# Layer 3 attention in steps of one key tile by eight heads, its halves split by token and turned just in time, TensorE in order

## The chip, the core and the metric

The kernel runs on one NeuronCore of a Trainium2 chip. Five engines work from queues of their own and meet at semaphores: TensorE (PE; its weight loads are listed as PEld), VectorE (DVE), ScalarE (ACT), GpSimd (POOL) and SyncE (SP, which issues DMAs). The metric is the device time of one execution in microseconds (us); smaller is better. Several executions give a median.

## The reference, cut to what matters

The program is four pairs of cross attention and feed-forward, run one after the other on x (4 batches of 256 tokens, 256 features) with a context of 4 x 1601 tokens. The change is in the last pair:

```python
def _L3_xattn_ref(x, context, Wq, Wk, Wv):        # 32 heads of 8
    q = (x @ Wq.T).reshape(b, n, 32, 8)
    kv = concatenate([context @ Wk.T, context @ Wv.T], -1).reshape(b, m, 32, 8, 2)
    k, v = kv[..., 0], kv[..., 1]
    q, k = _rmsnorm(q), _rmsnorm(k)               # over the 8 of a head
    attn = softmax(einsum('bhnd,bhmd->bhnm', q, k) * 8 ** -0.5)
    return einsum('bhnm,bhmd->bhnd', attn, v)
...
x = x + _L3_xattn_ref(_layernorm(x), ctx_2048, Wq, Wk, Wv)
x = x + _L3_ffn_ref(_layernorm(x), w_gate, w_up, w_down)
```

The feed-forward rounds weights to -1, 0, 1 and activations to whole numbers up to 127, and is 256 to 1024 to 256.

## The kernel before

P is 128 partitions, S 256 tokens, M 1601 context tokens in NM = 13 key tiles (the last of ML = 65 rows), B 4 batches, HD3 8.

**Heads on the array.** A head has only 8 features, so a score product uses 32 rows of the array: four runs of the head's 8, in which K and Q are split into a high part (upper bits) and the rest, so that the four pairs of parts are summed and the product keeps its accuracy in the fp32r type. Four heads lie in the four row groups of 32 and run side by side. `kT` and `qT` hold the normed K and Q turned to features by tokens, two tiles of 16 heads each (index `h`). For round `u` of four, `runs` (L1966 to L1974) takes 4 heads of the 16: a stream shuffle copies each head's 8 rows four times (L1971), two masks with per-partition bits make the part to subtract and the rest (L1972, L1973, VectorE), and GpSimd subtracts them into `kb` or `qb` (L1974). `spread` does so for a round in pieces of 256 columns, the next round's while this one runs.

**A step** is two key tiles by four heads (`pairs`, seven steps a round, the last of one tile). `scores` (L1987) makes eight products of 32 rows, 128 columns out and 256 tokens into two `s` tiles of 1024 columns (two PSUM banks each, three buffers go round), and ScalarE makes two exponentials `e` of them (L1998). `values` (L2002) multiplies the previous step's `e` by `va`: V with a column of ones after each head's 8, of which 32 columns are taken, in the four column groups side by side, into `o` (one buffer); these are plain fp32 and each appears as two matrix instructions in the trace. After a round, VectorE copies `o` to `os` (L2112), and `close` (L2012) turns it, divides by the sum that the ones gave, and GpSimd adds it to x (L2025).

**Side work.** `beside` (L2027) is a generator that the loop advances once a step: the K and V projection of the next batch (`l3_kv`, L1706: per key tile two fp32 products of 512 columns, four matrix instructions, then copies by VectorE; squares, norms; then the turning of all of K to `kT`, L1751), the next batch's queries (L1818), for batch 0 the rounding of the feed-forward weights (L1868), and the feed-forward of the batch before (`ffn`, L1911). They share one PSUM bank (`bank`, L1791). Batch 0's own K, V and `kT` are made during the layer 2 feed-forward; eleven key tiles of batch 1 while batch 0's queries are prepared (`FIRST3`). Layer 2's result is added to x for batches 1 to 3 by `l2_add` just before the loop, pinned on VectorE.

**Order.** The framework schedules every engine's queue from its own estimate; what is passed to `pin` (L118, `keep_in_program_order`) keeps its program order. In this stretch nothing of TensorE is pinned. All helper products are recorded under L79 (`mm`). The loop is L2082 to L2120; after it come the last `close` and the feed-forward of batch 3 (L2131 on).

Of the kernel before, what the change touches and what calls it, by code (L numbers as in the profile page):

```python
# [24 lines left out]
P = 128  # L25
# [32 lines left out]
VW3 = 16 * (HD3 + 1) + 24  # L58


class Kernel:
    def __init__(self, ctx, tc, ins, out):
        self.ctx, self.tc, self.nc = ctx, tc, tc.nc
        self.i, self.out = ins, out
        self.flip = 0
        self.hold = False
        self.flip4 = 0
# [10 lines left out]
    def mm(self, out, lhsT, rhs, start, stop, **kw):  # L78
        self.nc.tensor.matmul(out, lhsT, rhs, start=start, stop=stop, **kw)  # L79
# [1595 lines left out]
    def l3_open(self, es):  # L1675
# [4 lines left out]
        self.low3 = self.a3.tile([P, 2], I32, name="low3")  # L1680
        self.rest3 = self.a3.tile([P, 2], I32, name="rest3")
        nc.gpsimd.iota(self.low3, pattern=[[0, 2]], base=0, channel_multiplier=1)
        for n, bit in enumerate((4, 3)):
            c = self.low3[:, n : n + 1]
            nc.vector.tensor_scalar(c, c, 31 - bit, 31, ALU.logical_shift_left, ALU.arith_shift_right)
        nc.vector.tensor_scalar(self.rest3, self.low3, HIGH, None, ALU.bitwise_or)
        nc.vector.tensor_scalar(self.low3, self.low3, HIGH, None, ALU.bitwise_and)
# [9 lines left out]
    def values3(self, pool):  # L1697

        va = [pool.tile([P, NM, VW3], F32, name="va3", bufs=2) for _ in range(2)]
        n = 16 * (HD3 + 1)  # L1700
        for t in va:
            self.nc.vector.memset(t[:, :, :n].rearrange("p m (h e) -> p m h e", e=HD3 + 1)[:, :, :, HD3:], 1.0)
            self.nc.vector.memset(t[:, :, n:], 1.0)
        return va

    def l3_kv(self, b, st, early):  # L1706
# [4 lines left out]
        pool = self.late3 if b % 2 else self.a3  # L1711
        kr = st["kr"] = self.a3.tile([P, NM, D], F32, name="kr3")
        va = st["va"] = self.va3[b % 2]
        ss = st["ss"] = self.a3.tile([P, (NM + 2) * NH3 + 2], F32, name="ss3")
        for m in range(NM):
# [4 lines left out]
            tp = tf.rearrange("p (h d c) -> p h d c", d=HD3, c=2)  # L1720
            copy(kr[:, m, :].rearrange("p (h d) -> p h d", d=HD3), tp[:, :, :, 0])
            for h in range(2):
                copy(
                    va[h][:, m, : 16 * (HD3 + 1)].rearrange("p (h e) -> p h e", e=HD3 + 1)[:, :, :HD3],
                    tp[:, h * 16 : (h + 1) * 16, :, 1],
                )
# [15 lines left out]
        for _ in range(1 if b else 3):  # L1742
            yield
        kT = st["kT"] = [pool.tile([P, MP], F32, name="kT3", bufs=2) for _ in range(2)]
        for m0 in range(0, NM, 4):
            for h in range(2):
                n = min(4, NM - m0)
                copy = nc.scalar.copy if early() else nc.vector.tensor_copy
                tp = self.take().rearrange("p (m k) -> p m k", k=P)
                for m in range(n):  # L1750
                    nc.tensor.transpose(tp[:, m, :], kr[:, m0 + m, h * P : (h + 1) * P], self.ident)  # L1751
                copy(kT[h][:, m0 * P : (m0 + n) * P], tp[:, :n, :].rearrange("p m k -> p (m k)"))
                yield

    def l3_squares(self, st, v, m0, early, pool=None):

        n = v.shape[1]
        sq = pool.tile([P, 1, D], F32, name="sqq3", tag="run3", bufs=3) if pool else self.a3.tile([P, 5, D], F32, name="sq3")
# [9 lines left out]
    def l3(self, first):  # L1768
# [10 lines left out]
        pairs = [tuple(range(m, min(m + 2, NM))) for m in range(0, NM, 2)]  # L1779
        with ExitStack() as es:  # L1780
# [3 lines left out]
            ps_s = es.enter_context(tc.tile_pool(name="a3s", bufs=3, space=PSUM))  # L1784
            ps = es.enter_context(tc.tile_pool(name="a3p", bufs=1, space=PSUM))
            ps_o = es.enter_context(tc.tile_pool(name="a3o", bufs=1, space=PSUM))
            low, rest, idb = self.low3.bitcast(U32), self.rest3.bitcast(U32), self.idb
# [30 lines left out]
            def queries(b, st, old=None, fill=lambda n: None):  # L1818
# [13 lines left out]
                fill(0)  # L1832
                tp = bank().rearrange("p (k q t) -> p k q t", k=2, q=2)
                for k in range(2):
                    for q in range(2):
                        nc.tensor.transpose(tp[:, k, q, :], xn[:, q, k * P : (k + 1) * P], self.ident)
# [8 lines left out]
                qr = one.tile([P, 2, D], F32, name="qr3")  # L1845
# [12 lines left out]
                yield  # L1858
                yield
                qT = st["qT"] = two.tile([P, 2, S], F32, name="qT3")  # L1860
                tp = bank().rearrange("p (h t) -> p h t", h=2)
                for h in range(2):
                    for q in range(2):
                        nc.tensor.transpose(tp[:, h, q * P : (q + 1) * P], qr[:, q, h * P : (h + 1) * P], self.ident)
                nc.vector.tensor_copy(qT, tp)
# [45 lines left out]
            def ffn(b, q, xn, take):  # L1911
# [10 lines left out]
                yield  # L1922
                tp = take(BF16)[:, : 2 * P].rearrange("p (k t) -> p k t", k=2)
                for k in range(2):
                    nc.tensor.transpose(tp[:, k, :], vb[:, k * P : (k + 1) * P], idb)
                xT = two.tile([P, 2, P], BF16, name="xqT3")
                nc.vector.tensor_copy(xT, tp)
                yield
                g = two.tile([P, I3], F32, name="g3")
                for c in range(0, I3, 512):  # L1930
# [7 lines left out]
                    yield  # L1938
# [4 lines left out]
                    yield  # L1943
                hs, r = scale_of(g, "hq3")
                yield
                nc.vector.tensor_scalar(g, g, r, RND, ALU.mult, ALU.add)
                yield
# [3 lines left out]
                yield  # L1951
                tp = take(BF16).rearrange("p (k t) -> p k t", t=P)
                for k in range(I3 // P):
                    nc.tensor.transpose(tp[:, k, :], hb[:, k * P : (k + 1) * P], idb)
                hT = two.tile([P, I3 // P, P], BF16, name="hT3")
                nc.vector.tensor_copy(hT, tp)
                yield
# [8 lines left out]
            def runs(out, v, u, n):  # L1966

# [326 lines left out]
```

## Time and profile before

| | |
|---|---|
| median of 12 runs | 2521.85 us (2513.15 to 2528.69) |
| profiled execution | 2526.49 us |
| its span | 2524.8 us, 45207 instructions |
| whole span, busy | PE 2341.3, DVE 1636.6, ACT 1297.7, POOL 1018.0 us |
| mean granted TensorE clock | 0.963 |
| first score product / last exponential start | 1929.0 / 2494.0 us |

The stretch of this attention, cut so that each piece holds one round of four heads (14 exponentials of the tile `e` each), in us:

| batch | round 1 | 2 | 3 | 4 | 5 | 6 | 7 | 8 |
|---|---|---|---|---|---|---|---|---|
| 0 | 33.70 | 18.70 | 14.10 | 15.60 | 15.50 | 15.40 | 13.60 | 13.60 |
| 1 | 22.60 | 26.30 | 21.20 | 19.90 | 13.30 | 16.70 | 15.50 | 15.20 |
| 3 | 19.70 | 15.10 | 17.70 | 14.30 | 13.50 | 15.00 | 13.60 | 13.10 |

Costs of single instructions there, from its groups by shape: exponential of 1024 columns 1031 ns (of 512: 600 ns), mask of 256 columns 424 and 377 ns, shuffle 442 ns, GpSimd's subtraction of 256 columns 763 ns, scaling of `kr` 2077 ns, squares 2321 ns, ScalarE's table load 1283 ns (eleven of them), tanh 690 ns. How to read it: "busy" is the time in which an engine had at least one instruction; a wait is named with the instruction that waited, an arrow, and what released it.

### The profile page before, as it was taken

The page shows a single profiled execution, that of the slowest core. Times are in us where ns is not written, and L with a number is a line of the kernel's source. Part 1 is how long each engine was busy: PE and PEld are TensorE (multiplying, and loading weights), DVE is VectorE, ACT ScalarE, POOL GpSimd, SP SyncE. Part 2 cuts the span into 40 slices and gives each one's busy share as a digit, 9 for nine tenths or more (in the row PEclk, how much of TensorE's full clock was granted, in tenths as well). Part 3 has the DMA queues.
Part 4 walks back from the last instruction along what each step waited for, and adds up shares of the span by engine and source line. Part 5 has one row for each costly group of instructions (what it writes and reads, how often), then busy time and mean ns, then how long its engine had stood idle before and what let it go on. Part 6 is the DMA issues. An engine that isn't in the chain of part 4 may idle for free.

```text
span 2524.8 us, 45207 instructions
## 1 busy us (share of the span) xinstructions
PE 2341.3 (93%) x15959; PEld 1436.7 (57%) x15959; DVE 1636.6 (65%) x3940; ACT 1297.7 (51%) x3000; POOL 1018.0 (40%) x1773
## 2 busy tenths in 40 slices
PE   8989987899899999999999999998997898898897
PEld 5778876667645555555555555555563443444443
DVE  5553534753577777777777777773325876868774
ACT  3334444533655555445555454442324785857885
POOL 1015645312445555555555555542102544434331
PEclk9999998989999999999999999998998898998998
DMA  7165575633721111111111111004212000000000
GB/s 253 49 198 172 172 150 158 215 98 110 221 66 48 49 48 48 49 48 48 48 49 48 43 43 47 22 1 170 87 67 67 18 18 28 4 3 2 6 6 5
DMA packets 96521, 188.33 MB, mean 75 GB/s; under 512 B 15450, under 2 KB 64346, under 8 KB 95099
## 3 DMA queue, kind: packets, MB, share of 16 engines
q1 hardware_dynamic: 80150, 146.50, 17.5%
q0 software_dynamic: 10416, 28.46, 5.0%
q10 hardware_dynamic: 5732, 10.49, 1.3%
q8 instruction: 130, 2.13, 0.4%
q14 instruction: 93, 0.75, 0.1%
HBM read 137.29 MB, written 48.11 MB: 73 GB/s over the span
## 4 chain that ended last, share of the span: by engine, by line
PE 74%; DVE 14%; issue 4%; POOL 3%; ACT 2%; DMA 2%; another core or an unknown queue 1%; SPq 0%; ACTq 0%; POOLq 0%; DVEq 0%
PE o L79 21%; PE s L79 18%; PE f2gu L79 3%; PE b L79 3%; PE f1gu L79 2%; PE f0gu L79 2%; PE acc L79 2%; PE fill L1260 2%; PE tpq L79 2%; PE tpkv L79 2%; PE av L79 2%; DVE hi L1972 2%; DVE run L1971 2%; PE f0y L79 2%; PE f2y L79 1%
## 5 line engine op out<-in xcount | busy, mean ns | idle before, releaser
L1520 ACT ACTIVATE p<-s,nmsm 128x448 f32<-128x448 f32 (+1 forms) x512 | 326.0, 643 | 372.6 <-PE s L79 243.4
L1998 ACT ACTIVATE e<-s 128x1024 f32<-128x1024 f32 (+1 forms) x448 | 398.0, 970 | 143.7 <-PE s L79 141.9
L79 PE MATMUL o<-pT,va 128*128 128x256 f32 (+2 forms) x1920 | 430.2, 376 | 5.8 <-DVE pT L1561 4.3
L79 PE MATMUL s<-kT,qT 128*32 128x448 f32 (+1 forms) x4096 | 428.1, 556 | 7.9 <-ACT kT L1492 7.7
L79 PEld LDWEIGHTS o<-pT,va 128*128 128x128 f32 (+1 forms) x1920 | 344.1, 190 | 126.4 <-issue 86.2
L1555 POOL TENSOR_SCALAR p<-p,rm 128x448 f32<-128x448 f32 (+1 forms) x512 | 323.1, 651 | 6.3
L79 PE MATMUL o<-e,va 128*32 128x256 f32 (+1 forms) x3328 | 283.4, 410 | 27.1 <-DVE os L2112 21.1
L1516 DVE TENSOR_REDUCE nmsm<-s 128x2 f32<-128x896 f32 (+1 forms) x256 | 287.3, 1123 | 8.0
L1561 DVE STREAM_TRANSPOSE pT<-p 128x896 f32<-128x896 f32 (+1 forms) x256 | 270.6, 1111 | 4.7 <-POOL p L1555 4.0
L79 PEld LDWEIGHTS s<-kT,qT 128*32 128x32 f32 x4096 | 120.5, 109 | 260.3 <-issue 238.7
L1548 POOL TENSOR_TENSOR rm<-em,tot 32x8 f32<-32x8 f32 x256 | 54.1, 212 | 397.1 <-DVE tot L1545 385.8
L1974 POOL TENSOR_TENSOR kb<-run,hi 128x256 fp32r<-128x256 f32 (+1 forms) x224 | 155.4, 705 | 121.2 <-DVE run L1973 119.6
L79 PEld LDWEIGHTS o<-e,va 128*32 128x32 f32 (+1 forms) x3328 | 105.8, 113 | 121.7 <-ACT e L1998 30.2
L1513 DVE TENSOR_TENSOR s<-s,mask 128x128 f32<-128x128 f32 (+1 forms) x256 | 84.2, 330 | 99.7 <-PE s L79 91.6
L79 PE MATMUL s<-qb,kb 32*128 32x256 f32 (+1 forms) x1664 | 131.8, 346 | 17.5 <-ACT e L1998 11.7
L79 PEld LDWEIGHTS s<-qb,kb 32*128 32x128 f32 (+1 forms) x1664 | 77.4, 189 | 112.4 <-issue 61.9
L475 POOL DMA_INDIRECT f0xr<-f0xd,f0src x95 | 90.8, 955 | 68.9 <-PE f0y L79 24.4
L1260 PE MATMUL fill<-wkc_early,ctxT 128*128 128x256 f32 (+1 forms) x444 | 108.9, 396 | 9.4 <-ACT va_early L1268 7.2
L1520 ACT ACTIVATION_READ_ACCUMULATOR p<-s,nmsm 128x1 f32 x512 | 101.3, 198 | 0.0
L1972 DVE TENSOR_SCALAR hi<-run,low 128x256 uint32<-128x256 uint32 (+1 forms) x256 | 100.2, 410 | 0.2
L1260 PEld LDWEIGHTS fill<-wkc_early,ctxT 128*128 128x128 f32 (+1 forms) x444 | 85.7, 197 | 25.1 <-ACT va_early L1268 8.3
L1974 POOL TENSOR_TENSOR qb<-run,hi 128x256 fp32r<-128x256 f32 x32 | 25.8, 808 | 174.7 <-PE s L79 108.5
(518 smaller groups left out, 3935.7 us busy)
## 6 DMA issues: line engine op xcount, KB each, us to landing
ctxT<-in_ctxT SPq DMA_DIRECT2D x9, 1664.0 KB
vd<-va_early SPq DMA_DIRECT2D x96, 128.0 KB
kd<-kT_early SPq DMA_DIRECT2D x48, 256.0 KB
kT<-kd SPq DMA_DIRECT2D x16, 768.0 KB
va<-vd SPq DMA_DIRECT2D x16, 768.0 KB
f0yd<-f0ys SPq DMA_DIRECT2D x95, 128.0 KB
wq<-in_l_wq SPq DMA_DIRECT2D x16, 512.0 KB
wo<-in_l_wo SPq DMA_DIRECT2D x16, 512.0 KB
```

Of the source, the lines that this page charges most:

```text
L79: self.nc.tensor.matmul(out, lhsT, rhs, start=start, stop=stop, **kw)
L475: nc.gpsimd.indirect_dma_start(out=t, out_offset=None, in_=xd[:, :], in_offset=bass.IndirectOffsetOnAxis(ap=src[:, n : n + 1], axis=0),)
L1260: ins = nc.tensor.matmul(tp[:rows, t, :], ctxT[u // NKV2][:, k, c0 : c0 + rows], w[u % NKV2][:, k, :], start=k == 0, stop=k == 1,)
L1513: nc.vector.tensor_tensor(sv, sv, mask[:, 2 * c : 2 * c + 2, : nt - CT, :].rearrange("p n t i -> p n (t i)"), ALU.add)
L1516: nc.vector.tensor_reduce(ms[:, 0, 2 * c : 2 * c + 2], s[:, :, : nt * 32], AX.X, ALU.max, negate=True)
L1520: nc.scalar.activation(p[:, n, : nt * 32], s[:, n, : nt * 32], AF.Exp, bias=ms[:, 0, e : e + 1], accum_out=ms[:, 1, e : e + 1],)
L1548: nc.gpsimd.tensor_tensor(r[32 * a : 32 * a + 32], e[:, a], tot, ALU.mult)
L1555: nc.gpsimd.tensor_scalar(p[:, n, : nt * 32], p[:, n, : nt * 32], r[:, e : e + 1], 1.0, ALU.mult, ALU.mult)
L1561: self.pin(nc.vector.transpose(pT[:, 2 * c : 2 * c + 2, :nt, :].rearrange("p n t i -> p n (t i)"), p[:, :, : nt * 32]))
L1972: nc.vector.tensor_scalar(t.bitcast(U32), a.bitcast(U32), low[:, n : n + 1], None, ALU.bitwise_and)
L1974: nc.gpsimd.tensor_tensor(out, a, t, ALU.subtract)
L1998: nc.scalar.activation(e[:kr, :, :n, :], s[t][:kr, :, :n, :], AF.Exp, scale=1.0 / math.sqrt(HD3))
```

## The change

Weights are reordered on the host (`by_group`) so that a group `g` of eight heads is contiguous in a token's row, and V follows K instead of alternating with it. K and Q stay by token (`kr`, `qr`, two buffers each); `kT` and `qT` are gone. `halves` splits a part (three or four key tiles, eight heads, 64 features) into high part and rest, side by side, with one mask on VectorE and one subtraction on GpSimd. `turned` transposes it on TensorE, and for each `u` of two, VectorE shuffles the four runs out of PSUM and GpSimd copies them to the fp32r tile. `feed` does the splitting one part ahead and the turning at the start of the part before. A step is one key tile by eight heads (`u` is now the inner index of the tiles `s` and `e`). `values` takes the 32 columns of `va` from two heads' 18 on, by `e` of both heads, 512 columns, into an `o` of 512; of each half of the columns the rows of one head are used. `close` covers eight heads. PSUM: `s` two buffers, the bank two, `o` two. `self.strict` pins all of TensorE from the loop's start to its end. The side work yields after each half of a key tile's projection, and a counter `room`, raised by RATE each step and lowered by turns, closings and units, says when it advances; the feed-forward's yields count 0.5 and end the step's share. The functions `runs`, `spread` and the masks by partition bits are removed.

```diff
+VW3 = 16 * (HD3 + 1) + 14
+PARTS = [(0, 4), (4, 7), (7, 10), (10, NM)]
+RATE = [1.2, 1.5, 1.5, 0.8]
...
     def mm(self, out, lhsT, rhs, start, stop, **kw):
-        self.nc.tensor.matmul(out, lhsT, rhs, start=start, stop=stop, **kw)
+        self.ordered(self.nc.tensor.matmul(out, lhsT, rhs, start=start, stop=stop, **kw))
+    def ordered(self, ins):
+        if self.strict:
+            self.pin(ins)
...
         for m in range(NM):
             tf = self.take()
             for k in range(2):
                 self.mm(tf, ctxT[:, k, m * P : (m + 1) * P], self.wkv3[:, k, :], k == 0, k == 1)
...
+                if k == 0 and not early():
+                    yield
+            copy(kr[:, m, :], tf[:, :D])
+            copy(
+                va[:, m, :, : 16 * (HD3 + 1)].rearrange("p g (h e) -> p g h e", e=HD3 + 1)[:, :, :, :HD3],
+                tf[:, D:].rearrange("p (g h d) -> p g h d", g=2, d=HD3),
+            )
...
+        st["kr"] = kr
```

In the attention's function (indentation cut):

```diff
-ps_s = es.enter_context(tc.tile_pool(name="a3s", bufs=3, space=PSUM))
-ps = es.enter_context(tc.tile_pool(name="a3p", bufs=1, space=PSUM))
-ps_o = es.enter_context(tc.tile_pool(name="a3o", bufs=1, space=PSUM))
...
+ps_s = es.enter_context(tc.tile_pool(name="a3s", bufs=2, space=PSUM))
+ps = es.enter_context(tc.tile_pool(name="a3p", bufs=2, space=PSUM))
+ps_o = es.enter_context(tc.tile_pool(name="a3o", bufs=2, space=PSUM))
...
+def halves(v, g, name, bufs):
+    n = v.shape[1]
+    t = two.tile([P, n if bufs == 1 else 4, P], F32, name=name, bufs=bufs)[:, :n]
+    tv = t.rearrange("p n (e c d) -> p n e c d", c=2, d=HD3)
+    vv = v[:, :, g * 64 : (g + 1) * 64].rearrange("p n (e d) -> p n e d", d=HD3)
+    nc.vector.tensor_scalar(tv[:, :, :, 0, :].bitcast(U32), vv.bitcast(U32), HIGH, None, ALU.bitwise_and)
+    nc.gpsimd.tensor_tensor(tv[:, :, :, 1, :], vv, tv[:, :, :, 0, :], ALU.subtract)
+    return t
+def turned(out, t, order):
+    n = t.shape[1]
+    tp = bank()[:, : n * P]
+    for k in range(n):
+        self.ordered(nc.tensor.transpose(tp[:, k * P : (k + 1) * P], t[:, k, :], self.ident))
+    for u in range(2):
+        row = two.tile([P, 4 * P], F32, name="row3")[:, : n * P]
+        nc.vector.stream_shuffle(
+            row, tp, [16 * u + (k % 16 if order else k // 16 * 8 + k % 8) for k in range(32)]
+        )
+        nc.gpsimd.tensor_copy(out[:, u, : n * P], row)
+def feed():
+    last = None
+    for b in range(B):
+        for g in range(4):
+            for c, (m0, m1) in enumerate(PARTS):
+                st = states[b]
+                now = m0, c, halves(st["kr"][:, m0:m1, :], g, "half3", 2)
+                if c == 0:
+                    now += (halves(st["qr"], g, "halfq3", 1),)
+                if last is not None:
+                    yield ready(*last)
+                last = now
+    yield ready(*last)
+def ready(m0, c, t, tq=None):
+    k = two.tile([P, 2, 4 * P], F32R, name="kb3")
+    turned(k, t, True)
+    if c == 0:
+        self.q3 = two.tile([P, 2, S], F32R, name="qb3")
+        turned(self.q3, tq, False)
+    return k, self.q3, m0
...
+def scores(k, q, m):
     s = [ps_s.tile([P, 2, 2, S], F32, name="s3") for _ in range(2)]
...
+    kr = ML if m[0] == NM - 1 else P
+    c = (m[0] - m[1]) * P
+    for u in range(2):
         for r in range(4):
             rows = slice(32 * r, 32 * r + 32)
...
+            self.mm(s[r // 2][:kr, r % 2, u, :], k[rows, u, c : c + kr], q[rows, u, :], True, True)
...
+def values(e, o, va, g, m, b):
+    kr = ML if m == NM - 1 else P
+    for r in range(4):
+        c = (4 * r + g % 2 * 2) * (HD3 + 1)
+        self.mm(
+            o[32 * r : 32 * r + 32, :], va[:kr, m, g // 2, c : c + 32],
+            e[r // 2][:kr, r % 2].rearrange("p u t -> p (u t)"), m == 0, m == NM - 1,
+        )
+def close(b, os, g):
+    tp = bank()
+    for k in range(4):
+        self.ordered(nc.tensor.transpose(tp[:, k * P : (k + 1) * P], os[:, k * P : (k + 1) * P], self.ident))
```

Order of side work and the loop:

```diff
+        for _ in range(2 * (NM - sum(FIRST3) if b == 0 else NM)):
             next(kv)
             yield
         qs = queries(b + 1, st, b - 1 if b else None)
...
+        for _ in range(3):
             next(qs)
             yield
         for _ in kv:
...
+self.strict = True
+starts = [m0 for m0, _ in PARTS]
 last = done = None
 for b in range(B):
...
+    side = beside(b, states[b + 1] if b + 1 < B else {})
+    room = 0.0
+    for g in range(4):
+        o = ps_o.tile([P, 2 * S], F32, name="o3")
+        for m in range(NM):
+            room = min(room + RATE[b], 2.0)
+            if m in starts:
+                k, q, m0 = kq
+            e = scores(k, q, (m, m0))
+            if m == m0:
+                if b + 1 < B and g == 3 and m == starts[2]:
+                    while "qr" not in states[b + 1] or "kr" not in states[b + 1]:
                         next(side)
...
+                kq = next(more, None)
+                room -= 0.8
+            if m == 2 and done is not None:
                 close(*done)
                 done = None
...
+                room -= 0.8
+            while room > 0.5:
+                w = next(side, self)
+                if w is self:
+                    break
+                room -= w or 1.0
+                if w:
+                    break
+            if last is not None:
+                values(*last)
+                if last[4] == NM - 1:
+                    os = two.tile([P, 2 * S], F32, name="os3")
+                    nc.vector.tensor_copy(os, last[1])
+                    done = (last[5], os, last[3])
+            last = (e, o, states[b]["va"], g, m, b)
...
+self.strict = False
+values(*last)
+os = two.tile([P, 2 * S], F32, name="os3")
```

## The prediction

> **What bounds the kernel now.** I read the page first, then the layer 3 attention cut at the first exponential of each batch (112 exponentials each), then that stretch's waits, then single steps in the timeline. All that the change touches runs from 1929.0, the first score product, to 2495.3: 566.3 us of 2524.8.
>
> ```profile
> core 0: us, PE busy (x) PEld busy (x) DVE busy (x) ACT busy (x) POOL busy (x), PEclk, DMA share, GB/s
> 1929.00:2069.20 140.20, 119.43 (x1318) 57.66 (x1322) 117.42 (x396) 105.69 (x120) 65.41 (x92) 0.87 0.09 29
> 2069.20:2219.90 150.70, 134.28 (x1398) 63.31 (x1402) 112.05 (x387) 106.15 (x121) 60.35 (x88) 0.93 0.04 14
> 2219.90:2373.30 153.40, 136.49 (x1415) 64.52 (x1418) 114.67 (x392) 106.16 (x121) 60.83 (x88) 0.96 0.01 3
> 2373.30:2495.30 122.00, 111.70 (x1332) 52.42 (x1332) 75.63 (x290) 103.51 (x120) 40.36 (x70) 0.97 0.02 5
> ```
>
> One batch a row, batch 0 first. No engine is full: ScalarE does 105 us in each, and the batches take 122 to 153. TensorE (85 to 91% busy) and VectorE (84% in batch 0) share the limit, and it moves. In the waits of that stretch ScalarE waits for the score products, and TensorE for the copy that empties `o` (the weight loads wait for it too) and for `kb`:
>
> ```profile
> ACT e L1998 <- PE s L79: 141.9, 104, 4.9
> PE o L79 <- DVE os L2112: 21.1, 17, 2.4
> PEld s L79 <- POOL kb L1974: 20.0, 32, 4.2
> ```
>
> **The price of a step.** A full step now is two key tiles by four heads; the new one is one key tile by eight. Both have eight score products of 256 columns, two exponentials of 128x1024, and values over 2048 columns. Their rows on TensorE, in time order:
>
> ```profile
> 1972.45 0.51 PE L79 MATMUL s<-qb,kb 32*128 32x256 f32 x8
> 1972.89 1.07 PE L79 MATMUL o<-e,va 128*32 128x256 f32 x16
> 1973.89 0.66 PE L1751 MATMUL b<-ident,kr 128*128 128x128 f32 x4
> 1974.47 0.51 PE L79 MATMUL s<-qb,kb 32*128 32x256 f32 x8
> ...
> 2082.82 1.98 PE L79 MATMUL b<-wkv,ctxT 128*128 128x512 f32 x4
> 2084.73 0.51 PE L79 MATMUL s<-qb,kb 32*128 32x256 f32 x8
> ```
>
> From start to next start: scores 0.44, values 1.00, four transposes 0.58, one key tile of the K/V projection 1.91. So a bare step costs TensorE 1.44. The rows of values already run four heads side by side; a product twice as wide halves the instructions (16 to 8 a step) and not the columns. I take 0 for it; the bounds are 0 and, if all weight loading counted, the 106 us of weight loads for `o` in the page spread over 208 steps, halved: 0.25 a step. The rows stand near 0: 16 products in 1.00, or 0.06 a product, with the loads of 0.11 each beside them.
>
> **What is lost: the third score buffer.** Now three tiles of `s` go round for two a step, so scores of the next step start while an exponential still runs. After the change there are two. The first half of the next scores needs the first exponential done, the second half the second; TensorE, in order, can't finish any score tile before. The loop is then: two exponentials, release, remaining score products, start of the next exponential.
>
> ```profile
> 1976.70 0.51 PE L79 MATMUL s<-qb,kb 32*128 32x256 f32 x8
> 1977.30 1.94 ACT L1998 ACTIVATE e<-s 128x1024 f32<-128x1024 f32 x2 [0.28 <-PE s L79]
> ...
> 1978.96 0.34 PE L79 MATMUL s<-qb,kb 32*65 32x256 f32 x4
> ...
> 1979.39 1.08 ACT L1998 ACTIVATE e<-s 65x512 f32<-65x512 f32 x2
> ...
> 2482.34 3.77 ACT L1998 ACTIVATE e<-s 128x1024 f32<-128x1024 f32 x4 [0.72 <-PE s L79]
> ...
> 2483.42 0.50 PE L79 MATMUL s<-qb,kb 32*128 32x256 f32 x4 [0.17 <-ACT e L1998]
> ```
>
> Two exponentials take 1.94. An exponential that began at 2482.34 and took 1.02 ended at 2483.36, and the products that waited for it start at 2483.42: release 0.06. From score products to the exponential it is 0.60 when all eight are to do (1976.70 to 1977.30), 0.43 when four are (1978.96 to 1979.39). Here four of eight remain, in two rounds, so I take 0.48. A step is 1.94 + 0.06 + 0.48 = 2.48, bounds 2.43 and 2.60. There are 4 x 4 x 13 = 208 steps: **515.8 us**. Batch 3 now averages 122.0 / 52 = 2.35 for the same work: it must get slower. Batches 1 and 2 average 2.90 and 2.95.
>
> **What is hidden in it.** TensorE needs 1.44 of 2.48, so about 1.0 a step of other TensorE work is free. In it lie: the turning, 64 K parts of three or four transposes and 16 Q parts of two, 240 transposes in place of the 90 that went through `kr` and `qr` inside the stretch (0.58 for four, so 0.46 for three and, by the `os` pair's 0.37, 0.95 where K and Q come together); the closings, 16 of four transposes in place of 32 of two; the feed-forward of the batch before. If that cover goes, turning alone is 48 x 0.46 + 16 x 0.95 = 37 us. The wait for `o` goes with the second `o` buffer.
>
> VectorE gives up its most costly rows and stops being a limit:
>
> ```profile
> L1972 DVE TENSOR_SCALAR hi<-run,low 128x256 uint32<-128x256 uint32 x222 | 90.2, 424 | 0.1
> L1971 DVE STREAM_SHUFFLE run<-kT 128x256 f32<-128x256 f32 x191 | 82.2, 442 | 0.0
> L1974 POOL TENSOR_TENSOR kb<-run,hi 128x256 fp32r<-128x256 f32 x191 | 143.5, 763 | 112.9 <-DVE run L1973 112.9
> ```
>
> Masks on tokens cover 960 columns for eight heads where two rounds of both masks covered 7428; shuffles cover 3840 against 3714. With 0.42 for 256 columns of mask and 0.44 for 256 of shuffle (0.23 for 65, so about 0.73 for 512), VectorE's part falls from 297 to about 125 of its 420. GpSimd subtracts 960 columns and copies 3840 where it subtracted 3714; by 763 ns for 256 columns that is at most 1.3 times its 181 us, by 651 ns for 448 (its other scaling, L1555) less than now. Both stay under 60% of the stage.
>
> **What sticks out of the 2.48.** The counter `room` admits the side work. *Projection:* 26 halves of 0.96 in batches 1 and 2 and 4 in batch 0. Followed by hand at 1.5 a step, less 0.8 for a turn or closing, 26 take 22 steps; in seven a half meets a turn or closing (about 0.4 over), in six two halves meet (1.44 + 1.91 = 3.35, 0.87 over): 8 us a batch, **17** with 1 for batch 0. *Feed-forward:* some units meet a double turn, **4**. *ScalarE:* tanh, squares, roots and table loads are 27 us of that stretch; the 0.54 between exponentials takes about half, **13** (0 to 27). *Waits in order:* TensorE can no longer pass a product that waits for VectorE or GpSimd, and queued behind it are values, the next scores and thus the next exponentials. Now such waits other than for `o` and `kb` come to some 23 us; with 37 groups of transposes more (80 + 16 for 27 + 32) and slack in quiet steps I take **15** (0 to 35). *Start:* the additions of layer 2 stand on VectorE ahead of the first parts, **5** (0 to 10); the first score comes some 3 earlier, as the transposes of batch 0 before it go and its chain on VectorE shortens; the wider last closing costs 1.
>
> *Clock:* **6** (0 to 15), from this:
>
> ```profile
> 2172.80:2176.20 3.40, 1.77 (x26) 0.88 (x22) 3.14 (x13) 3.40 (x4) 2.04 (x3) 1.00 0.01 2
> 2176.20:2179.60 3.40, 3.40 (x34) 1.56 (x30) 2.93 (x16) 1.07 (x2) 2.25 (x5) 0.51 0.02 5
> ```
>
> After 3.4 us with TensorE busy 52% the granted clock was 0.51 for as long. The new bare step is 1.44 of 2.48, 58%, close above that; a cold stretch makes it 2.88, 0.4 over, and I count about 15. The Trainium skill (TensorE: Matmul & The Clock Gate, "The HAM clock gate") has the clock halved only after a whole idle window of about 3.4 us; by that rule this term would be 0 and the sum 6 less, but the row shows the drop with TensorE busy for half the window, so the row decides.
>
> **Sum.** 515.8 + 17 + 4 + 13 + 15 + 5 - 3 + 1 + 6 = 573.8 against 566.3: 7.5 longer. The profiled execution took 2526.49, with 1.7 outside its span, and becomes 2534; it lies 4.6 above the median, so on the median's scale it is 2521.85 + 7.5 = 2529.4, say 2530.
>
> **Rivals.** *The slack swallows nearly all* (faster): cycle 2.43, so 505.4, projection 17, ScalarE 6, waits 5, clock 3, start and end -2: 534, 32 less, **2490**. For it: VectorE's load and the `o` wait are gone, the counter spreads the work, and heads with projection now take 20 to 27 us against 16 of the new loop. Against: it needs every bound at its good end. *Turning comes too late* (slower): at the last part of a group, three steps, 7.4 us, must hold transposes 0.95, shuffles 2 x 0.73 + 2 x 0.44, and GpSimd copies, 2 x 1.5 + 2 x 0.76 by its worst row, partly side by side: about 6.3. A GpSimd operation of 2.1 or 2.3 us ahead (kr scaling, squares) or a busy VectorE pushes it past, and from then on each of 16 group starts is late by about 2: 32 more, **2562**. Against: the other parts need only 4 to 5. *The clock falls in the bare steps* of batches 0 and 3: some 80 steps x 0.45 = 36 more, **2566**. Against: batch 3 now holds 0.97, though with denser steps. That the wide product isn't four abreast I exclude: its four output positions are those of now.
>
> **Chances.** Forecast 0.50, its own range 2512 to 2550; slack swallows all 0.28; late turning 0.12; clock 0.10. A measurement here can't tell less than 0.2% (5 us) from no change. Of the forecast's half, 0.28 is slower by more, 0.14 within, 0.08 faster. So faster 0.08 + 0.28 = 0.36, same 0.14, slower 0.28 + 0.12 + 0.10 = 0.50. All good bounds together would give 2481, all bad ones about 2603; I leave out the ends: 2490 to 2574.
>
> **What would show it.** The loop: back-to-back bare steps at 2.4 to 2.6, ScalarE waiting about 0.5 once a step for `s`, batch 3 near 130 or more, batches 1 and 2 near 143. Waits: few on `os`, a few us on `kb`; more than 30 for `kb` means late turning. VectorE near 250 in the stage. A clock under 0.9 in batch 3 means the clock rival. Bare steps at 2.0 would make the loop itself wrong, and with it the forecast.

## The result and the profile after

The changed kernel takes 2550.34 us (median of 10 runs, 2547.34 to 2557.5) against 2523.84 (43 runs): a ratio of 1.0112, 95% interval 1.01 to 1.0124. It is 26.5 us slower; the forecast was 7.5 slower, 2530, and the result lies inside the range of 2490 to 2574. The profiled execution, which is not among the ten, is longer than all of them: 2561.5 us, 11 over the median. What follows takes it apart and says where that matters.

Engine totals of the page after, span first:

```profile
span 2559.8 us, 41292 instructions
...
PE 2366.4 (92%) x14415; PEld 1396.2 (55%) x14415; DVE 1480.3 (58%) x3240; ACT 1300.6 (51%) x2936; POOL 960.7 (38%) x1724
```

VectorE lost 156 us and GpSimd 57 against before, 3915 instructions are gone, and the time still grew. What the change was to relieve, it relieved. The stretch of this attention, one batch a row (columns: stretch, its length, busy time of PE, PEld, DVE, ACT and POOL, then the granted clock):

```profile
1929.00:2079.50 150.50, 127.15 (x931) 48.78 (x931) 66.82 (x187) 107.72 (x112) 44.12 (x75) 0.85 0.08 26
2079.50:2233.10 153.60, 138.78 (x1026) 52.16 (x1024) 74.95 (x210) 107.09 (x113) 47.03 (x75) 0.93 0.04 14
2233.10:2386.70 153.60, 138.76 (x1026) 52.25 (x1024) 74.46 (x208) 107.09 (x113) 46.99 (x75) 0.93 0.01 3
2386.70:2529.60 142.90, 122.58 (x960) 45.59 (x954) 49.71 (x158) 107.23 (x112) 28.95 (x59) 0.89 0.01 3
```

Batch 0 went from 140 to 150, batch 3 from 122 to 143, the two in the middle moved little (150.7 and 153.4 to 153.6 each). VectorE is at 35 to 49% in every batch: its load is no limit now. The clock is the column to look at: 0.87 to 0.85, 0.93 to 0.93, 0.96 to 0.93, 0.97 to 0.89.

The loop itself, two steps from the timeline (start, length, engine, operation; in brackets the idle time before and what ended it):

```profile
2470.72 0.68 PE L82 MATMUL s<-qb,kb 32*128 32x256 f32 x8
...
2471.40 1.94 ACT L2008 ACTIVATE e<-s 128x1024 f32<-128x1024 f32 x2 [0.56 <-PE s L82]
2471.81 1.06 PE L82 MATMUL o<-e,va 128*32 128x512 f32 x8
...
2472.80 0.38 PE L82 MATMUL s<-qb,kb 32*128 32x256 f32 x2
...
2473.39 0.50 PE L82 MATMUL s<-qb,kb 32*128 32x256 f32 x6 [0.21 <-ACT e L2008]
...
2473.90 1.94 ACT L2008 ACTIVATE e<-s 128x1024 f32<-128x1024 f32 x2 [0.55 <-PE s L82]
```

ScalarE starts at 2471.40 and again at 2473.90: 2.50. Two exponentials are 1.94; then 0.55 of nothing. In that gap six of the eight score products run, which had waited for a score buffer to be released. In the kernel before, with three buffers, the steps at full clock without side work on TensorE or ScalarE (58 of them) take 1.80 to 1.83 from one step's first exponential to the next; there four exponentials ran on for 3.77 without a gap (the row at 2482.34 in the prediction). So a step of the same work went from 1.82 to 2.49. Values take 0.99 from start (2471.81) to the next start (2472.80).

The waits of the stretch (engine, line, what ended it: us in total, times, longest):

```profile
POOL kb L1971 <- DVE row L1968: 304.2, 60, 9.2
PEld s L82 <- ACT e L2008: 203.8, 238, 4.1
ACT e L2008 <- PE s L82: 165.4, 195, 3.8
...
PE s L82 <- ACT e L2008: 58.6, 136, 3.9
```

TensorE waits for exponentials to free `s`, ScalarE waits for TensorE to fill it: each waits for the other in turn. The 304 us on GpSimd are idle time of an engine that has little to do. No wait of TensorE on `kb` is in the list; those on `qb` and on `os` are at most 3.2 and 1.5 us in all.

### The profile page after: what moved, and what is told of

The parts are those of the page before. It is cut to its first block, busy times and chain, and to the rows that moved or that the text cites. A ratio compares the mean times of both kernels' runs of the same rounds, so it can differ in the third digit from the quotient of the medians.

```text
span 2559.8 us, 41292 instructions
## 1 busy us (share of the span) xinstructions
PE 2366.4 (92%) x14415; PEld 1396.2 (55%) x14415; DVE 1480.3 (58%) x3240; ACT 1300.6 (51%) x2936; POOL 960.7 (38%) x1724
## 4 chain that ended last, share of the span: by engine, by line
PE 76%; issue 7%; ACT 6%; DVE 6%; DMA 2%; POOL 1%; SPq 0%; ACTq 0%; PEld 0%; DVEq 0%; POOLq 0%; PEldq 0%
PE o L82 21%; PE s L82 20%; ACT e L2008 4%; PE f2gu L82 3%; PE b L82 3%; PE f1gu L82 2%; PE fill L1267 2%; PE acc L82 2%; PE tpq L82 2%; PE f0gu L82 2%; PE av L82 2%; PE tpkv L82 2%; PE f0y L82 1%; PE f2y L82 1%; DMA f0xr<-f0xd,f0src 1%
## 5 line engine op out<-in xcount | busy, mean ns | idle before, releaser
L2008 ACT ACTIVATE e<-s 128x1024 f32<-128x1024 f32 (+1 forms) x416 | 403.4, 1020 | 165.7 <-PE s L82 165.4
L82 PEld LDWEIGHTS s<-qb,kb 32*128 32x128 f32 (+1 forms) x1664 | 92.9, 196 | 289.8 <-ACT e L2008 203.8
L82 PE MATMUL o<-e,va 128*32 128x512 f32 (+1 forms) x1664 | 250.4, 675 | 0.1
L82 PE MATMUL s<-qb,kb 32*128 32x256 f32 (+1 forms) x1664 | 160.7, 365 | 64.7 <-ACT e L2008 58.6
L1971 POOL CAST kb<-row 128x384 fp32r<-128x384 f32 (+1 forms) x128 | 68.6, 543 | 305.0 <-DVE row L1968 304.7
L1968 DVE STREAM_SHUFFLE row<-b 128x384 f32<-128x384 f32 (+2 forms) x160 | 88.6, 593 | 0.4
L82 PE MATMUL f2gu<-f2wgu,f2xsT 128*128 x176 | 85.5, 611 | 0.6 <-ACT f2xsT L79 0.3
```

What stands on the lines that cost most here:

```text
L82: self.ordered(self.nc.tensor.matmul(out, lhsT, rhs, start=start, stop=stop, **kw))
L1968: nc.vector.stream_shuffle(row, tp, [16 * u + (k % 16 if order else k // 16 * 8 + k % 8) for k in range(32)])
L1971: nc.gpsimd.tensor_copy(out[:, u, : n * P], row)
L2008: nc.scalar.activation(e[:kr], s[t][:kr], AF.Exp, scale=1.0 / math.sqrt(HD3))
```

## The experiments

All compare with the kernel before on the same chip. "Stage" is from the first score product to the end of the last value product in the profiled execution; "half clock" is the time in that stage with a granted clock of one half. A bare step is one in which TensorE has nothing to do but scores and values; a turn is the transposing of a part of K or Q, a closing that of `os`; steps are measured from first exponential to first exponential. e8, e9a and e9b ran on a chip where the kernel before takes 2478.8 us, the others where it takes 2521; ratios are what to compare.

| kernel | median us | ratio to before [95%] | stage us | half clock us |
|---|---|---|---|---|
| before | 2523.84 | 1 | 566.3 | 78.5 |
| after | 2550.34 | 1.0112 [1.01, 1.0124] | 600.2 | 116.0 |
| e2_pairs_first | 2500.8 | 0.9927 [0.9901, 0.9953] | 548.3 | 47.8 |
| e3_before_two_s | 2594.23 | 1.0292 [1.0268, 1.0316] | 633.0 | 99.0 |
| e1_free_order | 2577.57 | 1.0218 [1.0195, 1.024] | 620.8 | 23.9 |
| e5_warm | 2535.2 | 1.0057 [1.0039, 1.0074] | 579.0 | 34.1 |
| e6_turn_twice | 2552.09 | 1.0125 [1.0107, 1.0143] | 594.9 | 75.1 |
| e4_three_s | 2552.45 | 1.0119 [1.0101, 1.0137] | 601.6 | 116.1 |
| e4b_three_s_apart | 2516.35 | 0.9987 [0.9976, 0.9998] | 558.4 | 81.9 |
| e7_three_s_pairs | 2557.41 | 1.0132 [1.0109, 1.0154] | 606.0 | 129.7 |
| e8_pairs_warm | 2470.81 | 0.9965 [0.9948, 0.9982] | 560.2 | 37.5 |
| e9a_apart_units | 2477.92 | 0.9994 [0.998, 1.0009] | 568.4 | 88.7 |
| e9b_apart_rate | 2481.53 | 1.0014 [1.0002, 1.0026] | 575.4 | 109.2 |

**Is it the two score buffers?** Two kernels ask that from both sides. The first keeps the two buffers and only lets the products of the first buffer come first:

```diff
-for u in range(2):
-    for r in range(4):
-        rows = slice(32 * r, 32 * r + 32)
+for u, r in ((u, r) for t in range(2) for u in range(2) for r in (2 * t, 2 * t + 1)):
+    rows = slice(32 * r, 32 * r + 32)
```

> The changed kernel with the eight score products of a step in another order: the four of the first score tile (two heads, both u), then the four of the second. Only two row groups run side by side then, so scores cost TensorE about 0.87 in place of 0.44 and a bare step 1.87. Two-buffer theory: the second half of the scores alone waits for the second exponential, the next first exponential follows at once, and a bare step falls from 2.49 to 1.85 to 2.0; TensorE becomes the bound with about 523 us of work, the stretch takes 540 to 560 in place of 600, the whole 2490 to 2515. Rival, the buffers aren't the limit (order, turning or clock are): bare steps stay at 2.4 or more and the time rises by the extra score time or stays, 2545 to 2600.

Measured: 2500.8, ratio 0.9927, faster than both kernels. The timeline of e2_pairs_first:

```profile
2433.94 1.06 PE L82 MATMUL o<-e,va 128*32 128x512 f32 x8
...
2434.10 3.75 ACT L2007 ACTIVATE e<-s 128x1024 f32<-128x1024 f32 x4 [0.70 <-PE s L82]
...
2435.18 0.45 PE L82 MATMUL s<-qb,kb 32*65 32x256 f32 x4 [0.17 <-ACT e L2007]
...
2436.09 0.45 PE L82 MATMUL s<-qb,kb 32*65 32x256 f32 x4 [0.47 <-ACT e L2007]
...
2438.07 1.94 ACT L2007 ACTIVATE e<-s 128x1024 f32<-128x1024 f32 x2 [0.22 <-PE s L82]
```

Four exponentials, two steps, now run without a gap from 2434.10: while the second exponential of a step runs, the first buffer is free, and its four products, which now stand together, fill it. In the changed kernel's order (by `u`, over both buffers) no buffer is full before the sixth product, and the third already waits for the second exponential. The bare steps that begin at full clock without other work on ScalarE, 62 of them, fell from 2.49 to between 1.82 and 2.20 (one 2.27).

The second takes the old kernel's third buffer away and changes nothing else:

```diff
-ps_s = es.enter_context(tc.tile_pool(name="a3s", bufs=3, space=PSUM))
+ps_s = es.enter_context(tc.tile_pool(name="a3s", bufs=2, space=PSUM))
```

> The kernel before with two score buffers in place of three, all else as it was. Two-buffer theory: a full step can't go under 2.49, so the quiet rounds of four heads rise from 13.6 to 16.0 or more (six full steps and a short one), batch 3 from 122 to 135 to 145, the whole to 2545 to 2575. Rival: the old schedule is limited by VectorE and the o wait anyway, and the time stays within 2515 to 2535.

Measured: 2594.23, that is 73 us slower. Sign as the theory has it, size well above it. Its timeline shows what else was lost:

```profile
2545.91 0.62 PE L79 MATMUL o<-e,va 128*32 128x256 f32 x2
...
2546.46 0.50 PE L79 MATMUL s<-qb,kb 32*128 32x256 f32 x4
...
2552.07 1.06 PE L79 MATMUL o<-e,va 128*32 128x256 f32 x14
...
2553.06 0.50 PE L79 MATMUL s<-qb,kb 32*128 32x256 f32 x4
```

With two buffers the framework put the sixteen value products of a step in two places, 2 and 14, in about a hundred steps. From start to next start the two take 0.55 and the fourteen 0.99, where all sixteen together took 1.00 before. So this run contains the missing buffer and a worse order, and does not price the buffer alone.

**What does the pinned order cost?** One line of the changed kernel is taken out:

```diff
-self.strict = True
```

> The changed kernel without the pin on TensorE's order in the loop; nothing else differs. Two-buffer theory: a bare step must stay at 2.49 us, since two score tiles go round whatever the order is; the whole stays within 2535 to 2565, and what waits TensorE could now pass (some 15 us by my sum) may come back. Rival, the order is what costs: the steps get shorter than 2.4 and the time falls to 2525 or below.

Measured: 2577.57, 27 us slower than the changed kernel, though the stage is hardly at half clock any more (23.9 us). So the pinned order is a gain here and no cost. The time lies outside both expectations, and the bare steps didn't stay at 2.49 whatever the order: some take 1.82, and more of them 2.8 to 3.2. What makes the long ones is in the timeline of e1_free_order:

```profile
2505.07 1.04 PE L82 MATMUL o<-e,va 65*32 65x512 f32 x2
...
2506.04 0.50 PE L82 MATMUL s<-qb,kb 32*128 32x256 f32 x4
...
2506.47 1.06 PE L82 MATMUL o<-e,va 65*32 65x512 f32 x6
...
2507.46 0.50 PE L82 MATMUL s<-qb,kb 32*128 32x256 f32 x4
```

The value products of four pairs of heads run side by side, all eight in 0.99. The framework's order puts one pair's two products apart from the other six: 0.97 for the two (2505.07 to 2506.04), 0.99 for the six (2506.47 to 2507.46). The step is then 2 x 0.98 + 2 x 0.43 = 2.82 of TensorE without a gap, and 2.83 is a common step length in batches 0 and 3 of that run. The values are split so in 104 of the 208 steps. The pinned program keeps the eight together. No run tests the split by itself, so how much of the 27 us it makes isn't shown.

**What does the clock cost?** Four transposes of the identity fill each step that has no other TensorE work:

```diff
+made = self.made          # self.made: products recorded by mm
 while room > 0.5:
...
+if self.made == made:
+    tp = bank()
+    for n in range(4):
+        self.ordered(nc.tensor.transpose(tp[:, n * P : (n + 1) * P], self.ident, self.ident))
```

> The changed kernel with four transposes of the identity (0.56 us of TensorE work whose result nobody reads) in every step that has no other TensorE work between scores and values. They fit in the 1.0 us that TensorE has free. Clock theory: 32 steps began at half clock and cost some 28 us over 2.49; with TensorE busy in every step the granted clock of the stretch goes from 0.85 to 0.93 up to 0.95 or more and 10 to 25 us come back: 2525 to 2542. Rival, the clock is an effect of stalls and not of bare steps: the clock stays and the time too, 2545 to 2560.

Measured: 2535.2, some 15 us below the changed kernel, for more work on TensorE. The rows of batches 0 and 3 of e5_warm, to hold against those of after:

```profile
1920.60:2062.00 141.40, 130.05 (x1026) 56.51 (x1026) 66.24 (x186) 107.12 (x112) 43.73 (x74) 0.94 0.09 28
...
2365.00:2499.60 134.60, 123.55 (x1032) 51.93 (x1031) 47.68 (x152) 104.75 (x110) 27.66 (x57) 0.99 0.01 3
```

The clock rises in both (0.85 to 0.94, 0.89 to 0.99); the whole stage is 21 us shorter, 579.0 against 600.2. What the half clock looks like in the changed kernel (rows before and during two drops, columns as above):

```profile
2490.34:2493.75 3.41, 2.28 (x23) 0.89 (x23) 0.00 (x0) 2.40 (x3) 0.06 (x1) 1.00 0.00 0
2493.75:2497.16 3.41, 3.41 (x23) 1.19 (x21) 1.70 (x5) 1.94 (x2) 1.00 (x2) 0.50 0.00 0
...
1988.58:1991.99 3.41, 2.42 (x22) 0.85 (x18) 0.00 (x0) 2.85 (x4) 0.00 (x0) 1.00 0.00 0
1991.99:2005.64 13.65, 13.40 (x73) 5.25 (x73) 8.62 (x21) 7.95 (x9) 2.77 (x6) 0.50 0.01 1
```

TensorE was busy for 67 and 71% of the 3.4 us before, with no pause over 0.6 us in it, and was then given half clock for 10.2 us (the row shows the first 3.4) and for 13.7 us. In the whole stage the clock dropped 20 times. Seven drops followed a pause of TensorE of 1.3 to 2.8 us; before the other 13 it had paused for at most 0.53 us and was busy for 66 to 83% of the 3.41 us. In e5_warm six drops are left, five of them after a pause of 1.3 us or more: with the bare steps filled, the drops that follow no stall are all but gone. The busy share alone doesn't tell when the clock drops: six other stretches of 3.41 us in the changed kernel, busy for 59 to 70%, were followed by none.

**Is the turning hidden?** The parts of the keys after the first are transposed twice over, some 20 us of TensorE more:

```diff
-for k in range(n):
+for k in list(range(n)) * times:      # times is 2 for the parts after the first
```

> After, with the transposes of the parts of the keys after the first made twice over, the second on top of the first: 96 transposes more at about 0.2 us each on TensorE, some 20 us of TensorE's time, nothing else changed, output the same. Theory (the turning goes where TensorE waits anyway for an exponential, about 1.0 us in each step): 0 to +8 us against after, median 2548 to 2560. Rival (turning is paid on the path): +15 to +22 us, median 2565 to 2575. A gain of a few us would mean that the extra products keep the clock up, as in e5_warm.

Measured: 2552.09, ratio 1.0125 against 1.0112, the two intervals on top of each other. The extra products may have kept the clock up (half clock 75 against 116 us), which could hide a cost in the total. The steps tell the two apart: those at full clock with a turn and no projection, query or feed-forward work exceed 2.49 by 0.4 us in all in the changed kernel (42 steps) and by 0.7 us with the transposes doubled (50 steps). So at full clock the turning is hidden, doubled too.

**Would three buffers have saved it?** The score buffer comes back, and the second bank and second `o` go:

```diff
-a3s bufs=2, a3p bufs=2, a3o bufs=2
+a3s bufs=3, a3p bufs=1, a3o bufs=1
...
-for _ in range(2 * (NM - sum(FIRST3) if b == 0 else NM)):
+for _ in range(NM - sum(FIRST3) if b == 0 else NM):
     next(kv)
-    yield
+    yield 2.0
```

> After, with three buffers for the scores as before, paid for with one buffer each for the products beside the loop and for the values' sums; the projection goes in whole tiles again. Nothing is left out. Theory (the bare step of 2.49 us is the two exponentials at 0.97 plus the 0.5 us of score products that stand between the release of a buffer and the next exponential, and that only because two buffers are all there are): bare steps fall to 1.82 to 2.0 us, bound by ScalarE; some of the gain is lost where the one remaining side buffer and the one buffer of sums make TensorE wait at turns and closings (some 16 closings at 1 to 2 us, 32 turns at 0.5 to 1 us: 30 to 60 us). Median 2480 to 2530, below after by at least 20 us. Rival (the step is held by TensorE's own work or by the order, not by buffers): bare steps stay at 2.4 us or more, median 2560 to 2610 because of the buffers taken away.

Measured: 2552.45, the same as after; the expected 2480 to 2530 was missed. Half of the theory held: of the 31 bare steps that begin at full clock, 28 take 1.81 to 1.83. The other half was far too small. The timeline of e4_three_s at a turn:

```profile
2166.83 0.66 PE L1963 MATMUL b<-ident,half 128*128 128x128 f32 x4
...
2169.13 0.41 PE L1963 MATMUL b<-ident,halfq 128*128 128x128 f32 x2 [1.65 <-DVE row L1966]
...
2170.53 1.03 PE L1934 MATMUL b<-idb,hb 128*128 128x128 bf16 x8 [0.99 <-DVE row L1966]
...
2174.25 1.94 ACT L2006 ACTIVATE e<-s 128x1024 f32<-128x1024 f32 x2 [5.24 <-PE s L82]
```

K's turn, Q's turn and a feed-forward unit ask for the one bank in a row, the later ones wait for VectorE to shuffle the one before out of it, and ScalarE stands for 5.24 us. Taking side work out of such steps, and allowing one unit a step elsewhere, tests that:

```diff
+apart = m == m0 or m == 2
...
-while room > 0.5:
+while room > 0.5 and not apart:
     w = next(side, self)
...
-    if w:
-        break
+    break
```

> As e4_three_s, and the steps that carry a turn or a closing take no other side work, which goes to other steps at one unit each, so that the single side buffer is asked for once a step. Theory: waits of TensorE on the side buffer shrink against e4_three_s, bare steps as there, median 10 to 30 us below e4_three_s. Rival (the side buffer costs little): within 5 us of e4_three_s, or slower by up to 20 us as the work that is pushed back no longer fits before the batch's end.

Measured: 2516.35, 36 us below e4_three_s, more than the 10 to 30 expected, and a hair under the kernel before. ScalarE's waits for scores fell from 171.5 to 127.9 us, and the wait of `mm`'s products beside the loop for the shuffles from 23.2 to 5.2. So meetings at the one bank ate most of the third buffer's gain. The half clock fell by 34 us as well (116.1 to 81.9), so not all of the 36 us need be the waits themselves. Two steps of 17.4 us at the ends of batches 1 and 2 were left, where the rest of the feed-forward ran in one piece. Two more kernels tried to spread it, the first with `if w: break` put back, the second also with RATE 2.0 for batches 1 and 2:

> As e4b_three_s_apart, but a unit of side work that uses no TensorE product no longer takes up a step's whole share, so that the feed-forward comes earlier. In e4b_three_s_apart batches 1 and 2 each end in one step of 17.4 us, in which the rest of the feed-forward runs with ScalarE waiting 11 us. Theory (that backlog is what holds e4b_three_s_apart back, not the buffers): those steps vanish and 15 to 30 us go, median 2485 to 2502 on the scale of before at 2521 (ratio 0.986 to 0.993). Rival (the same waits come back at other steps): within 8 us of e4b_three_s_apart.

> As e9a_apart_units, with the counter raised by 2.0 a step in batches 1 and 2 in place of 1.5. Theory: the projection, a whole tile of 1.9 us, then enters every step that is free of turns and closings, which makes those steps 3.35 us each as in e4_three_s, and gives the time back later as bare steps of 1.82: within 6 us of e9a_apart_units, with no step over 8 us at the end of a batch. Rival (a backlog is still the limit in e9a_apart_units): 10 us or more below it.

Measured: ratios 0.9994 and 1.0014, no gain over e4b's 0.9987; the 0.986 to 0.993 expected of the first was missed. The end steps only shrank to 14.2 and 14.4 us, and to 13.1, so the backlog was not removed and its price stays unmeasured.

**Do the gains add?** Both edits of order, e4 and e2 together (diffs as above):

> As e4_three_s with the score products of a step in the order of their buffers (the first buffer's four, then the second's), as in e2_pairs_first. Theory (both edits take away the same half microsecond behind the release of a buffer): bare steps 1.82 to 1.95 as in e4_three_s, and no more than 15 us between the two kernels. Rival (the two gains add up): 30 us or more below the better of e4_three_s and e2_pairs_first, median under 2470.

Measured: 2557.41 against 2552.45, no gain: with three buffers, pairing buys nothing, as it removes the same gap. And e2 with the extra transposes of e5:

> e2_pairs_first and e5_warm together: the score products in the order of their buffers, and four transposes of the identity in each step that has no other work for TensorE. Nothing is left out. Theory (two separate costs: 0.5 us behind the release of a buffer, and the products at half clock, of which e2_pairs_first still has 14 steps with 15 us over 2.49 us each): the gains add in part, median 2485 to 2500, that is 0 to 15 us below e2_pairs_first. Rival (with a step of 1.8 to 2.2 us TensorE has no room left, and four transposes of some 0.2 us lengthen the step): 2505 to 2530.

Measured: ratio 0.9965 against e2's 0.9927, stage 560.2 against 548.3. The rival was right in kind: half clock fell by 10 us only (47.8 to 37.5), and quiet steps that took 1.82 and 2.20 by turns take some 2.03 to 2.15 and 2.4 to 2.6. The two ratios were taken on different chips and their intervals just meet, so that the filling did harm isn't certain; that it gained nothing is. In these two pairs filling work paid where TensorE had room and the clock was lost, and not elsewhere.

## Why the prediction was right, and where its sizes were off

Stated first what has to be explained: in the profiles the stage grew by 33.9 (600.2 against 566.3), where the sum had 10.5 (7.5 and the 3 of the earlier start; 1 of this, the wider last closing, lies behind the stage). The execution profiled after began the stage at 1929.4; seven others with the same code ahead of it, but for a third buffer in three of them (e1, e2, e4, e4b, e5, e6, e7) began at 1916.2 to 1923.8, 1920.2 on average, against 1929.0 before (and 1927.7 in e3, which has the old code there). So the usual balance is +33.9, -8.8, and +0.7 behind the stage: 25.8, against 26.5 in the medians.

- **The loop, 2.48 a step, 515.8: held.** 2.49 to 2.50 measured, against 1.82 with three buffers before. e4 shows that it is the two buffers (1.82 again with three), e2 that it is how they are filled: a mere order of products takes 0.3 to 0.67 from it. What I did not see is that the same two buffers need not cost this; the price is for filling both at once.
- **Wide value product at 0, second `o` buffer: held.** 0.99 a step, as before; TensorE waits 1.5 us for `os` in all.
- **Turning hidden: held at full clock.** Doubled it costs nothing measurable, and a double turn of K and Q alone takes 2.49. "Turning comes too late" falls: no wait of TensorE for `kb` is in the list.
- **VectorE, 250 for the stage: 265.5.** GpSimd 166.7, where it had 226.9.
- **Projection 17: 17.5**, over 46 steps (a step's excess over 2.49, sorted by what else runs in it).
- **ScalarE's other work 13: 19.3**, in 17 steps. Two table loads of 1.28 around one other activation fall inside one step, which then takes 4.9 to 6.1, and the 0.54 between exponentials hides little of that.
- **Waits in order and feed-forward units, 15 and 4: 15.1 together**, within the bounds of the sum. But the reasoning behind the 15 is not confirmed: it treated the pinned order as a cost only, and with the order left free the value products are split and the kernel is 27 slower. What does cost is a double turn that meets another product for the side buffers: six such steps take 4.28 to 5.78, 13.7 over 2.49 in all (two of them, of 4.28, also hold a tanh and are counted to ScalarE; the two longest run partly at half clock). For units of the feed-forward that meet one the sum had 4; four of the six are such, and 10.1 over. No wait on the additions of layer 2, for which it had 5, is in the list.
- **Clock 6 (0 to 15): the term that failed.** I counted some 15 steps begun at half clock at 0.4 each. There were 32, and they exceed 2.49 by 28.3 in all, 0.88 each. The ten of them without other TensorE work average 2.70, only 0.21 over; it is the others that cost: four with a closing average 3.58, three with a turn of three 3.56. At half clock the 1.0 us that hid turns and closings is gone, so work that is free at full clock stands on the path. I had priced the clock for bare steps alone, and the cover of the turning for full clock alone. Each step stands under one heading only, so 28.3 is rough: the longest of the 32 (6.93, 4.4 over) also holds two table loads, and steps in which the clock drops midway are counted elsewhere. e5, which gives most of it back, is 15 us faster in the median and 21 in the stage.
- **Start -3: about -9** on average, with the larger size in the favourable direction.

So the stage's miss is 33.9 - 10.5 = 23.4: clock +22, ScalarE +6, waits -4, the rest about -1 (sizes rounded, within 2 of the whole). In the medians, 2550.34 lies 20 above the forecast of 2530, at the very end of the forecast's own range of 2512 to 2550, and only 16 below the clock rival's 2566. The direction and the mechanism, a third buffer given up for a wait in every step, were right, and no luck. That the time came out no higher is in part luck: waits 4 below the sum and a start 6 earlier than forecast made up for some of the clock. In the list of what would show it, "batch 3 near 130, batches 1 and 2 near 143" was missed by 10 to 13 each, and "a clock under 0.9 in batch 3 means the clock rival" came true at 0.89: the result lies between my forecast and that rival, which had 36 us for it. The clock term is also where a row and a rule disagreed beforehand, and these runs decide for the row: with TensorE busy for 67% of 3.41 us and no pause over 0.6 us the clock still halved, and the term that the rule would have put at 0 was the one most in need of being larger. The rule is that of the Trainium skill (TensorE: Matmul & The Clock Gate, "The HAM clock gate"), which has the clock halved after a whole idle window of about 3.4 us. The same section also tells of a kernel whose clock swung because TensorE paused briefly and often between groups of matmuls, which is nearer to what these runs show.

The likeliest faster case ("the slack swallows nearly all") needed every term at its good end, and four were not: the clock stood some 25 above what it assumed, ScalarE's work 13, the waits 10, and a step of 2.49 in place of 2.43 makes another 12.

## What to carry to other kernels

With two buffers between two engines, order the producer's work so that one buffer is finished before the other is begun; spreading it over both makes each release worth nothing until the last. A third buffer paid here only when what it was taken from (the one bank for side work) was not asked for several times in a step, and even then less than the order did with two. And where products run side by side in the array's column groups, keep the group together: a split set took 0.97 and 0.99 here in place of 0.99. Cover that is counted at full clock must be counted at half clock too: a closing or a turn of three, free in a step of 2.49, made it 3.5 to 3.8.

## What the runs showed of the hardware

- In the changed kernel's stage the granted clock halved 13 times after 3.41 us in which TensorE was busy for 66 to 83% and never paused for more than 0.53 us, and stayed so for 3.4 to 13.7 us, always a multiple of 3.41. What decides it is open: six stretches busy for 59 to 70% were followed by no drop. Four transposes in each step without other work were enough to raise the mean from 0.89 to 0.99 in batch 3.
- Value products in different column groups overlap so fully that two of eight take 0.97 and all eight 0.99.
- The first score product, under the same code ahead of it (but for a third buffer in three), came between 1916.2 and 1929.4 in eight executions: 13 us of spread before the change's stage begins, which is half of the difference to be explained. A term of a few us is best read from the stage's own length.
